# A product of the selective scan moved from VectorE to GpSimd, with B spread by loads from a DRAM copy

## The chip, the cores and the metric

The kernel runs on one core of a Trainium2 chip. The metric is the device time of one execution in microseconds: 5143.98 before the change, the median of three runs (5142.33 to 5146.24). The profile shown was taken of one execution, whose first to last instruction span 5146.1 us.

A core has five engines, each with a queue of its own that it works through in order: TensorE (PE in the profile; its weight loads are PEld), VectorE (DVE), ScalarE (ACT), GpSimd (POOL) and SyncE (SP), which here only issues transfers. SBUF is the working memory with 128 partitions, PSUM the memory that TensorE writes its sums into (eight banks of 128 x 512 f32), DRAM lies outside the core.

## The reference

The input is a batch of 8 images, 384 channels, 32 x 32 pixels, all in f32. Layer 0 normalises over channels, runs a selective scan (Mamba) over the 1024 pixels forward and backward, adds a gated depthwise 3 x 3 convolution and the input. Layer 1 is causal attention with rotary embedding and a feed-forward whose weights are Kronecker products. What the change touches is the scan:

```python
x_dbl = jnp.einsum('blc,ec->ble', u, x_proj_w)
dt, Bm, Cm = jnp.split(x_dbl, [dt_rank, dt_rank + D_STATE], axis=-1)
delta = jax.nn.softplus(jnp.einsum('blr,dr->bld', dt, dt_proj_w) + dt_proj_b)
A = -jnp.exp(A_log)
deltaA = jnp.exp(delta[..., None] * A)
deltaBu = (delta * u)[..., None] * Bm[:, :, None, :]

def step(h, inp):
    dA, dBu, c = inp
    h = dA * h + dBu
    return (h, jnp.einsum('bdn,bn->bd', h, c))
```

There are 16 state dimensions n. For each of them and each channel d, a recurrence runs over the tokens; B and C hold one number per token and n, the same for all channels.

## The kernel before

The kernel goes through the batch element by element. In layer 0 the channels lie on the partitions (384 = 3 groups of 128, called cc) and the tokens along the free dimension; in layer 1 tokens lie on the partitions. The scan of an element has four steps, each over a half of the tokens (512): forward first half, forward second half, backward second half, backward first half. Within a step `scan` loops over the 16 state dimensions, so that there are 8 x 4 x 16 = 512 state dimensions in all. For each one:

- ScalarE computes da = exp(delta A), three instructions (L331).
- VectorE computes hs = du * bb, one instruction over 3 x 512 elements (L333). du is delta times u; bb is row n of B, the same on every partition.
- VectorE runs the recurrence in place of hs, one `tensor_tensor_scan` for each channel group (L341). It reads da and hs, both in SBUF. In the first steps of each direction the last state is saved (L344).
- VectorE multiplies hs by cb, row n of C on every partition (L345).
- TensorE adds hs into the PSUM tile y with an identity as weights (L349); a product of f32 matrices shows as two records, so there are six for the three groups.

bb and cb come from TensorE: the tile bc holds B and C with tokens on the partitions, and four transposes of a column that is repeated 128 times make the row on all partitions, in PSUM (`spread`, L320). There is one PSUM bank for bb and one for cb, three for y and three for everything else (the tiles named w).

The work that doesn't belong to the running scan is written as generators, of which `pump` advances some pieces after each state dimension: the next step's `prepare` (the short convolution L256 and L264, B and C, and delta through a softplus, L292 to L302), the next element's `norm_in`, the gated convolution `local` (L213 to L231), and the previous element's attention and feed-forward (`tail`, three pieces at a time). The framework then orders each engine's instructions by its own estimate, so in the built program the recurrences of one state dimension are mixed with the product with C of the one before and with side work. GpSimd has, within the loop, only the copies of L499 for the feed-forward. SyncE issues the loads of x and the stores of the output.

Buffers that matter here: hs has three, da two (each for three groups), du one, dl (delta) two, tmp (work tiles of one group, in the softplus, the norm and `local`) four.

Of the kernel before, what the change touches and what calls it, by code (L numbers as in the profile page):

```python
"""Two layers of a vision backbone on one NeuronCore, batch element by batch element.

Layer 0 (bidirectional selective scan and gated depthwise convolution) works with channels on the
partitions; layer 1 (causal attention with rotary embedding, Kronecker-factored feed-forward) with
tokens on the partitions.  What an element needs stays in SBUF from its load to its store.

The scan runs in four steps for each element: forward over the first and the second half of the
tokens, then backward over the second and the first.  The work that does not belong to the scan
(the next step's projections, the next element's norm and input projection, the previous
element's layer 1) is issued in pieces between the state dimensions of the running step.  # L10
"""

# [13 lines left out]
P = 128  # L26
HB = 512  # tokens of a half
STEPS = [(0, 0), (0, 1), (1, 1), (1, 0)]  # (direction, half) in the order of the scan


@with_exitstack
def conv_attn_kernel(
# [29 lines left out]
    NF = cp1T.shape[0] // P  # L62
    NG = P // NJ  # row groups of the feed-forward's first factor
    NT = HB // P  # token tiles of a half
    HR = HB // W  # image rows of a half

# [4 lines left out]
    ps_b = ctx.enter_context(tc.tile_pool(name="ps_b", bufs=1, space=bass.MemoryType.PSUM))  # L71
    ps_w = ctx.enter_context(tc.tile_pool(name="ps_w", bufs=3, space=bass.MemoryType.PSUM))

# [8 lines left out]

    # ---------------------------------------------------------------- x comes first
    xv = x.rearrange("b (cc p) h w -> b p cc (h w)", p=P)
# [9 lines left out]

    # ---------------------------------------------------------------- constants and weights
    ident = const.tile([P, P], F32, name="ident")
# [33 lines left out]

    # A = -exp(A_log)
    nc.scalar.activation(nega, nega, AF.Exp)
    nc.vector.tensor_scalar_mul(nega, nega, -1.0)

    # D as diagonals
    ddiag = const.tile([P, NC, P], F32, name="ddiag")
    for cc in range(NC):
        nc.gpsimd.tensor_scalar(ddiag[:, cc], ident, v_d[:, cc : cc + 1], None, ALU.mult)

    # q, k weights with their rotated columns beside them  # L140
    qk = []
# [11 lines left out]
    sscale = 1.0 / K**0.5  # L153
    # sums the two stacked halves and gives the sum to both
    fold = const.tile([P, P], F32, name="fold")
# [3 lines left out]
    make_causal_mask(nc, cmask, -1e30)  # L159
    # the second factor of the feed-forward's output  # L160
    emat = const.tile([NJ, NJ, NI], F32, name="emat")
# [6 lines left out]

    # ---------------------------------------------------------------- layer 0: norm and input
    xn_t, u_t = {}, {}  # L170

    def norm_in(b, h):
# [9 lines left out]
        for cc in range(NC):  # L182
            nc.scalar.square(xn[:, cc, cols], xt[:, cc])
            nc.tensor.matmul(ms, ones, xn[:, cc, cols], start=cc == 0, stop=cc == NC - 1)
        rstd = l0.tile([P, HB], F32, tag="tmp", name=name("rstd"), bufs=4)
        nc.scalar.activation(rstd, ms, AF.Sqrt, bias=eps[:, 0:1], scale=1.0 / C)
# [17 lines left out]
    def local(b):  # L204
        """x + res_scale * sigmoid(dwconv(xn)) * xn, in place of x."""
        xn = xn_t[b]
        for cc in range(NC):
            img = xn[:, cc].rearrange("p (h w) -> p h w", w=W)
            for h in range(2):
                cols = slice(h * HB, (h + 1) * HB)  # L210
                sg = l0.tile([P, HB], F32, tag="tmp", name=name("sg"), bufs=4)
                sv = sg.rearrange("p (h w) -> p h w", w=W)
# [21 lines left out]
    def gate(b, h):  # L234
        """silu(z) of a half."""
        sz = l0.tile([P, NC, HB], F32, tag="sz", name=name("sz"))
        for m in range(NC):
            pz = bank()
            for cc in range(NC):
                nc.tensor.matmul(  # L240
                    pz, win[:, cc, C + m * P : C + (m + 1) * P],
                    xn_t[b][:, cc, h * HB : (h + 1) * HB],
                    start=cc == 0, stop=cc == NC - 1,
                )
            nc.scalar.activation(sz[:, m], pz, AF.Silu)
        return sz

    # ---------------------------------------------------------------- layer 0: the scan
    def prepare(b, step, res):
        """u after the convolution, B and C, delta of a step."""  # L250
        d, h = step
# [22 lines left out]
        yield  # L274
        # B and C with tokens on the partitions, from where transposes spread them
        pt = bank()
        for i in range(NT):
            nc.tensor.transpose(
                pt[:, i * NX : (i + 1) * NX], xd[:, i * P : (i + 1) * P], ident[:NX, :NX]
            )  # L280
        bc = l0.tile([P, NT, 2 * NS], F32, tag="bc", name=name("bc"), bufs=2)
        nc.scalar.copy(bc, pt[:, : NT * NX].rearrange("p (i e) -> p i e", i=NT)[:, :, R:])
        yield
        # softplus(v) = relu(v) + ln(1 + exp(-|v|))
        dl = l0.tile([P, NC, HB], F32, tag="dl", name=name("dl"), bufs=2)
        sps = []
        for cc in range(NC):
            pd = bank()
            nc.tensor.matmul(pd, dtw[:, cc * P : (cc + 1) * P], xd[:R], start=True, stop=True)
            sp = l0.tile([P, HB], F32, tag="tmp", name=name("sp"), bufs=4)  # L290
            bias = v_dtb[:, cc : cc + 1]
            nc.scalar.activation(sp, pd, AF.Abs, bias=bias)  # L292
            nc.scalar.activation(dl[:, cc], pd, AF.Relu, bias=bias)
            sps.append(sp)
            yield
# [5 lines left out]
        for cc, sp in enumerate(sps):  # L301
            nc.vector.tensor_add(dl[:, cc], dl[:, cc], sp)  # L302
        res.append((uc, bc, dl))

    carry = const.tile([P, NS, NC], F32, name="carry")

    def scan(step, prep, y, first, last, save, restore, pump):
        """One step: y += C . h + D u over the half's tokens."""
        d, h = step
        uc, bc, dl = prep  # L310
        du = l0.tile([P, NC, HB], F32, tag="du", name=name("du"))
        nc.vector.tensor_mul(du, dl, uc)
        for cc in range(NC):
            nc.tensor.matmul(y[:, cc], ddiag[:, cc], uc[:, cc], start=first, stop=False)  # L314

        def spread(what, at):
            """A column of bc as a row on every partition."""
            pb = ps_b.tile([P, HB], F32, tag=what, name=name(what))
            for i in range(NT):
                nc.tensor.transpose(  # L320
                    pb[:, i * P : (i + 1) * P],
                    bc[:, i, at : at + 1].to_broadcast([P, P]),
                    ident,
                )
            return pb.unsqueeze(1).to_broadcast([P, NC, HB])

        bb, cb = spread("bb", 0), spread("cb", NS)
        for n in range(NS):
            da = l0.tile([P, NC, HB], F32, tag="da", name=name("da"), bufs=2)
            for cc in range(NC):  # L330
                nc.scalar.activation(da[:, cc], dl[:, cc], AF.Exp, scale=nega[:, cc, n : n + 1])  # L331
            hs = l0.tile([P, NC, HB], F32, tag="hs", name=name("hs"), bufs=3)
            nc.vector.tensor_mul(hs, du, bb)  # L333
            if n + 1 < NS:
                bb = spread("bb", n + 1)
            for cc in range(NC):
                o, a = hs[:, cc], da[:, cc]
                if d:
                    o, a = o[:, ::-1], a[:, ::-1]
                init = carry[:, n, cc : cc + 1] if restore else 0.0  # L340
                nc.vector.tensor_tensor_scan(o, a, o, init, ALU.mult, ALU.add)  # L341
# [4 lines left out]
            if n + 1 < NS:  # L346
                cb = spread("cb", NS + n + 1)
            for cc in range(NC):
# [5 lines left out]
    def project(b, h, yz, t1):  # L354
        """The layer's output, tokens on the partitions: yz @ out_proj.T + x'."""
        for i in range(NT):
# [10 lines left out]

    # ---------------------------------------------------------------- layer 1
    def token_norm(t1, ti0):
        """1 / sd and -mean / sd of a half's tokens."""  # L370
        mv = l1.tile([P, NT, 2], F32, tag="mv", name=name("mv"))
# [20 lines left out]
    def attention(b, t1):  # L392
        k_all = l1.tile([P, L], F32, tag="k", name=name("k"))
        v_all = l1.tile([P, L // P, C], F32, tag="v", name=name("v"))
        for hh in range(2):
# [4 lines left out]
            for i in range(NT):  # L400
# [10 lines left out]
                yield  # L411
            # q as (q cos, q_rot sin), one above the other; k as their sum, twice
            def turned(w, nm):
# [74 lines left out]
    def feed_forward(b, t1):  # L488
        for hh in range(2):
            nrm = token_norm(t1, hh * NT)  # L490
            yield
            # the Kronecker factors' short dimension first, copied to each row group
            px = bank()
# [44 lines left out]

    # ---------------------------------------------------------------- the order of it all
    def run(gen):  # L540
# [7 lines left out]
    def pump_of(gens, each):  # L548
        """Advances the generators by so many pieces between two state dimensions."""

# [68 lines left out]
def _arrays(i):  # L619
    """The inputs, transposed and packed for the loads, and the table of rotary angles."""  # L620
    import numpy as np
# [67 lines left out]
```

## Time and profile before

| what | value |
|---|---|
| median of three runs | 5143.98 us (5142.33 to 5146.24) |
| the profiled execution's span | 5146.1 us |
| VectorE busy | 4576.4 us, 89% |
| TensorE busy | 4037.1 us, 78% |
| ScalarE busy | 2710.1 us, 53% |
| GpSimd busy | 37.1 us, 1% |
| product with C (L345), the last one's end | 4930.5 us |
| the four steps of a middle element | about 165, 176, 135 and 144 us |

How to read the profile. A group's line names the source line, the engine, the operation, the tile written and those read, the shapes and the number of instructions; then the group's busy time in us and the mean ns of one; then the engine's idle time just before these instructions and who ended most of it. The chain follows the work back from the end: at each step to what released an instruction, or to the one before it on its engine. A line of the windows view gives one stretch: its borders, its length, then busy us and number of instructions for PE, PEld, DVE, ACT and POOL, TensorE's granted clock, and the transfers' share. In the timeline the first number is the start in us, the second the duration. Records of neighbouring VectorE instructions overlap by some 0.08 us, so sums over records are a little higher than busy times.

### The profile page before, as it was taken

To read this page: it belongs to the slowest core of one execution; us is meant where nothing else is said; L and a number is where in the kernel's file an instruction comes from. 1 tells how busy PE (TensorE), PEld (TensorE's weight loads), DVE (VectorE), ACT (ScalarE), POOL (GpSimd) and SP (SyncE) were. 2 spreads that over 40 slices of the span, in tenths; PEclk is the share of its full clock that TensorE was granted. 3 is DMA by queue.
4 is the path that set the end of the run, shared out by engine and by line. 5 is a ranking of instruction groups with operands and counts; after the bars stand their busy time and mean duration, and the time that the engine had idled before them with its cause. 6 is when DMAs were issued, how large, how long until landed. Compare 5 with 4: busy or idle time off the path is not lost.

```text
span 5146.1 us, 35644 instructions
## 1 busy us (share of the span) xinstructions
PE 4037.1 (78%) x12656; PEld 1932.0 (38%) x12656; DVE 4576.4 (89%) x4788; ACT 2710.1 (53%) x3879; POOL 37.1 (1%) x75
## 2 busy tenths in 40 slices
PE   6667788778887788867888678877788777887677
PEld 2333343334433344333443334433343333433332
DVE  7998999989999899998998988998999989999841
ACT  4643557635575345744467445664456635575222
POOL 0000000000000000000000000000000000000000
PEclk8879899898988999999998899989999898988988
DMA  1000000000000000000000000000000000000000
GB/s 41 0 0 6 7 1 7 6 6 7 1 6 7 6 7 1 13 0 7 7 1 13 0 7 7 1 13 6 6 1 6 7 6 7 1 6 6 1 0 13
DMA packets 19255, 31.11 MB, mean 6 GB/s; under 512 B 5356, under 2 KB 6276, under 8 KB 19076
## 3 DMA queue, kind: packets, MB, share of 16 engines
q1 hardware_dynamic: 17152, 28.64, 1.6%
q8 instruction: 99, 1.62, 0.1%
q14 instruction: 80, 0.66, 0.0%
q10 hardware_dynamic: 1924, 0.19, 0.0%
HBM read 16.24 MB, written 12.58 MB: 6 GB/s over the span
## 4 chain that ended last, share of the span: by engine, by line
DVE 60%; PE 22%; issue 10%; ACT 8%; DMA 0%; ACTq 0%; POOL 0%; DVEq 0%; POOLq 0%
DVE hs L341 27%; DVE hs L333 11%; DVE hs L345 11%; PE y L349 4%; DVE uc L264 3%; PE w L360 3%; DVE sg L222 2%; PE w L240 2%; PE w L518 2%; PE w L479 2%; ACT da L331 2%; PE y L314 1%; PE w L512 1%; PE w L432 1%; ACT L331 1%
## 5 line engine op out<-in xcount | busy, mean ns | idle before, releaser
L349 PE MATMUL y<-hs,ident 128*128 128x512 f32 x3072 | 1637.3, 673 | 80.7 <-DVE hs L345 80.7
L331 ACT ACTIVATE da<-dl,nega 128x512 f32<-128x512 f32 x1536 | 1019.9, 714 | 1246.5 <-DVE hs L341 1052.8
L345 DVE TENSOR_TENSOR hs<-hs,cb 128x1536 f32<-128x1536 f32 x512 | 892.1, 1742 | 152.0 <-PE cb L320 146.9
L341 DVE TENSOR_TENSOR_SCAN hs<-da,carry,hs 128x512 f32<-128x512 f32 x768 | 937.6, 1265 | 8.6 <-ACT da L331 6.1
L341 DVE TENSOR_TENSOR_SCAN hs<-da,hs 128x512 f32<-128x512 f32 x768 | 900.8, 1209 | 3.6 <-ACT da L331 0.4
L333 DVE TENSOR_TENSOR hs<-du,bb 128x1536 f32<-128x1536 f32 x512 | 889.1, 1737 | 16.6 <-PE bb L320 16.3
L349 PEld LDWEIGHTS y<-hs,ident 128*128 128x128 f32 x3072 | 625.5, 219 | 710.0 <-issue 617.6
L320 PE MATMUL cb<-ident,bc 128*128 128x128 f32 x2048 | 370.5, 308 | 469.2 <-DVE hs L345 468.0
L320 PE MATMUL bb<-ident,bc 128*128 128x128 f32 x2048 | 336.9, 287 | 292.8 <-DVE hs L333 291.4
L320 PEld LDWEIGHTS cb<-ident,bc 128*128 128x128 f32 x2048 | 251.4, 151 | 668.4 <-DVE hs L345 593.0
L331 ACT ACT_TABLE_LOAD x275 | 352.8, 1283 | 246.3 <-DVE hs L341 213.1
L320 PEld LDWEIGHTS bb<-ident,bc 128*128 128x128 f32 x2048 | 237.1, 141 | 589.5 <-DVE hs L333 456.2
L222 DVE SCALAR_TENSOR_TENSOR sg<-xn,dww,sg 128x496 f32<-128x496 f32 (+3 forms) x384 | 273.3, 715 | 1.5
L479 PE MATMUL w<-v,pT 128*128 128x384 f32 x576 | 224.6, 540 | 27.5 <-ACT pT L475 27.5
L518 PE MATMUL w<-gl,cp1s 128*32 128x512 f32 x384 | 208.1, 658 | 37.9 <-ACT gl L517 36.8
L264 DVE SCALAR_TENSOR_TENSOR uc<-u,cw,uc 128x512 f32<-128x512 f32 (+3 forms) x288 | 210.6, 737 | 1.3
L512 PE MATMUL w<-xrT,fc1s 32*128 32x512 f32 x384 | 161.2, 686 | 39.7 <-ACT xrT L507 39.7
L479 PEld LDWEIGHTS w<-v,pT 128*128 128x128 f32 x576 | 114.8, 207 | 113.5 <-ACT pT L475 41.9
L360 PE MATMUL w<-wout,sz 128*128 128x384 f32 x384 | 140.1, 502 | 20.6 <-DVE sz L607 11.9
L517 ACT ACT_TABLE_LOAD x106 | 136.0, 1283 | 29.8 <-PE w L512 28.4
L517 ACT ACTIVATE gl<-w 128x512 f32<-128x512 f32 x192 | 107.5, 595 | 77.5 <-PE w L512 76.5
L267 ACT ACTIVATE uc<-uc 128x512 f32<-128x512 f32 x96 | 59.7, 629 | 151.7 <-DVE uc L264 151.4
(122 smaller groups left out, 3869.7 us busy)
## 6 DMA issues: line engine op xcount, KB each, us to landing
x<-in_x_dram SPq DMA_DIRECT2D x16, 768.0 KB, 4.5
out_dram<-os SPq DMA_DIRECT2D x48, 256.0 KB, 2.0
win<-in_in_wT_dram SPq DMA_DIRECT2D x1, 1152.0 KB, 9.1
wout<-in_out_wT_dram SPq DMA_DIRECT2D x1, 576.0 KB, 7.4
wvs<-in_wv_dram SPq DMA_DIRECT2D x1, 576.0 KB, 4.9
cs<-in_rope_dram SPq DMA_DIRECT2D x1, 512.0 KB, 4.9
fc1s<-in_fc_dram SPq DMA_DIRECT2D x1, 192.0 KB, 3.4
cp1s<-in_cp1T_dram SPq DMA_DIRECT2D x1, 192.0 KB, 2.8
```

Source lines behind the costliest of these rows:

```text
L222: nc.vector.scalar_tensor_tensor(o, img[:, r0 + dy : r1 + dy, c0 + dx : c1 + dx], dww[:, cc, k : k + 1], o, ALU.mult, ALU.add,)
L264: nc.vector.scalar_tensor_tensor(o, u[:, cc, a + s : e + s], cw[:, cc, k : k + 1], o, ALU.mult, ALU.add)
L320: nc.tensor.transpose(pb[:, i * P : (i + 1) * P], bc[:, i, at : at + 1].to_broadcast([P, P]), ident,)
L331: nc.scalar.activation(da[:, cc], dl[:, cc], AF.Exp, scale=nega[:, cc, n : n + 1])
L333: nc.vector.tensor_mul(hs, du, bb)
L341: nc.vector.tensor_tensor_scan(o, a, o, init, ALU.mult, ALU.add)
L345: nc.vector.tensor_mul(hs, hs, cb)
L349: nc.tensor.matmul(y[:, cc], ident, hs[:, cc], start=False, stop=last and n == NS - 1)
L360: nc.tensor.matmul(po[:, :C], yz[:, cc, cols], wout[:, cc], start=cc == 0, stop=False)
L479: nc.tensor.matmul(pa[:, :C], pT[:, j * P : (j + 1) * P], v_all[:, j], start=j == 0, stop=j == ti,)
L517: nc.scalar.activation(gl, ph, AF.Gelu)
L518: nc.tensor.matmul(po[:NJ], cp1s[:, f], gl, start=f == 0, stop=f == NF - 1)
```

## The change

The product of du and B goes to GpSimd, which works in SBUF alone; so B has to be spread over the partitions in SBUF. `prepare` stores the 16 rows of B of a step (xd, with tokens along the free dimension) to a DRAM tile bd, and `scan` loads two rows at a time onto all 128 partitions (bbt, two buffers, 512 KB for each load). The transposes for bb go. du is computed at the end of `prepare` of the step ahead and has two buffers. The bank that bb had goes to the side work (three to four). For room in SBUF, tmp goes from four buffers to three, bc holds C alone, and da becomes a tile for each group with four buffers. In the changed file comments are gone, and lines are moved by a few.

```diff
+NB2 = 2
-    ps_w = ctx.enter_context(tc.tile_pool(name="ps_w", bufs=3, space=bass.MemoryType.PSUM))
+    dram = ctx.enter_context(tc.tile_pool(name="dram", bufs=1, space=bass.MemoryType.DRAM))
+    ps_w = ctx.enter_context(tc.tile_pool(name="ps_w", bufs=4, space=bass.MemoryType.PSUM))
...
-        rstd = l0.tile([P, HB], F32, tag="tmp", name=name("rstd"), bufs=4)
+        rstd = l0.tile([P, HB], F32, tag="tmp", name=name("rstd"), bufs=3)
...
+        bd = dram.tile([NS, HB], F32, tag="bd", name=name("bd"), bufs=2)
+        nc.sync.dma_start(bd, xd[R : R + NS])
...
-        bc = l0.tile([P, NT, 2 * NS], F32, tag="bc", name=name("bc"), bufs=2)
-        nc.scalar.copy(bc, pt[:, : NT * NX].rearrange("p (i e) -> p i e", i=NT)[:, :, R:])
+        bc = l0.tile([P, NT, NS], F32, tag="bc", name=name("bc"), bufs=2)
+        nc.scalar.copy(bc, pt[:, : NT * NX].rearrange("p (i e) -> p i e", i=NT)[:, :, R + NS :])
...
-        res.append((uc, bc, dl))
+        du = l0.tile([P, NC, HB], F32, tag="du", name=name("du"), bufs=2)
+        nc.vector.tensor_mul(du, dl, uc)
+        res.append((uc, bc, bd, dl, du))
...
-        uc, bc, dl = prep
-        du = l0.tile([P, NC, HB], F32, tag="du", name=name("du"))
-        nc.vector.tensor_mul(du, dl, uc)
+        uc, bc, bd, dl, du = prep
...
-        bb, cb = spread("bb", 0), spread("cb", NS)
+        cb = spread(0)
         for n in range(NS):
-            da = l0.tile([P, NC, HB], F32, tag="da", name=name("da"), bufs=2)
-            for cc in range(NC):
-                nc.scalar.activation(da[:, cc], dl[:, cc], AF.Exp, scale=nega[:, cc, n : n + 1])
+            if n % NB2 == 0:
+                bbt = l0.tile([P, NB2, HB], F32, tag="bb", name=name("bb"), bufs=2)
+                nc.sync.dma_start(
+                    bbt, bd[n : n + NB2].rearrange("(o k) t -> o k t", o=1).to_broadcast([P, NB2, HB])
+                )
+            das = []
+            for cc in range(NC):
+                da = l0.tile([P, HB], F32, tag="da", name=name("da"), bufs=4)
+                nc.scalar.activation(da, dl[:, cc], AF.Exp, scale=nega[:, cc, n : n + 1])
+                das.append(da)
             hs = l0.tile([P, NC, HB], F32, tag="hs", name=name("hs"), bufs=3)
-            nc.vector.tensor_mul(hs, du, bb)
-            if n + 1 < NS:
-                bb = spread("bb", n + 1)
+            nc.gpsimd.tensor_mul(hs, du, bbt[:, n % NB2].unsqueeze(1).to_broadcast([P, NC, HB]))
             for cc in range(NC):
-                o, a = hs[:, cc], da[:, cc]
+                o, a = hs[:, cc], das[cc]
```

## The prediction

> **What bounds the kernel now.** I read the shares by engine first, then the chain of waits, then the groups, then stretches of one batch element.
>
> ```profile
> span 5146.1 us, 35644 instructions
> ...
> PE 4037.1 (78%) x12656; PEld 1932.0 (38%) x12656; DVE 4576.4 (89%) x4788; ACT 2710.1 (53%) x3879; POOL 37.1 (1%) x75
> ...
> DVE 60%; PE 22%; issue 10%; ACT 8%; DMA 0%; ACTq 0%; POOL 0%; DVEq 0%; POOLq 0%
> ...
> L345 DVE TENSOR_TENSOR hs<-hs,cb 128x1536 f32<-128x1536 f32 x512 | 892.1, 1742 | 152.0 <-PE cb L320 146.9
> L341 DVE TENSOR_TENSOR_SCAN hs<-da,carry,hs 128x512 f32<-128x512 f32 x768 | 937.6, 1265 | 8.6 <-ACT da L331 6.1
> L341 DVE TENSOR_TENSOR_SCAN hs<-da,hs 128x512 f32<-128x512 f32 x768 | 900.8, 1209 | 3.6 <-ACT da L331 0.4
> L333 DVE TENSOR_TENSOR hs<-du,bb 128x1536 f32<-128x1536 f32 x512 | 889.1, 1737 | 16.6 <-PE bb L320 16.3
> ```
>
> VectorE is busy 89% and carries 60% of the chain; GpSimd is empty. Three quarters of VectorE's time are the scan's own: the product with B (L333), three recurrences (L341), the product with C (L345). The windows below are the four scan steps of the third element, in order, with the bare tail last.
>
> ```profile
> core 0: us, PE busy (x) PEld busy (x) DVE busy (x) ACT busy (x) POOL busy (x), PEclk, DMA share, GB/s
> 1350.00:1516.00 166.00, 142.50 (x456) 66.94 (x455) 152.68 (x186) 119.81 (x169) 4.43 (x8) 0.92 0.01 5
> 1516.00:1692.00 176.00, 132.06 (x392) 57.35 (x391) 167.16 (x162) 95.44 (x125) 0.00 (x0) 0.88 0.01 5
> 1692.00:1828.00 136.00, 105.19 (x333) 52.16 (x334) 118.45 (x95) 62.99 (x89) 0.00 (x0) 0.92 0.02 6
> 1828.00:1972.00 144.00, 120.29 (x408) 64.10 (x408) 133.18 (x156) 65.33 (x108) 0.00 (x0) 0.94 0.02 6
> ...
> 4930.00:5146.00 216.00, 166.40 (x467) 74.16 (x466) 39.58 (x106) 61.58 (x118) 3.08 (x8) 0.85 0.02 8
> ```
>
> In each step VectorE is the fullest engine. Its idle time is 13.3 + 8.8 + 17.5 + 10.8 = 50.4 us per element, 403 us for eight.
>
> **What GpSimd does beside VectorE.** This is the row that decides for me. The only GpSimd work in the loop is a small copy (L499). Two places from the timeline, GpSimd first, then VectorE at the second of them:
>
> ```profile
> 862.16 0.30 POOL L499 COPY xr<-xr 128x128 f32<-128x128 f32 x1 [0.63 <-DVE xr L498]
> ...
> 739.05 1.16 POOL L499 COPY xr<-xr 128x128 f32<-128x128 f32 x1 [2.04 <-DVE xr L498]
> ```
> ```profile
> 738.90 1.22 DVE L341 TENSOR_TENSOR_SCAN hs<-da,hs 128x512 f32<-128x512 f32 x1
> ```
>
> At 862.16 VectorE runs L333, whose second operand lies in PSUM, and the copy takes 0.30. At 739.05 it runs a recurrence, with both operands in SBUF: the copy ends at 740.20, 0.09 after the recurrence (740.12). Of the 64 copies, 26 meet no VectorE instruction with two SBUF operands and take 0.294 to 0.298; the other 38 (L341, L222, L496) all end 0.09 to 0.16 after it. So GpSimd does not read while such an instruction runs, and it does get in between two back-to-back recurrences. The recurrence behind the copy took 1.246 against 1.195 for the one after it: a hint that VectorE waits in its turn, no proof, as the copy is so short.
>
> **The change part by part.**
>
> *The product with B leaves VectorE.* 512 x 1.737 = 889 us, and the 17 us it waited for bb: -906. TensorE loses 512 x 4 transposes (337 us) and their weight loads; they lie beside VectorE's work: 0. With no cover left, a step could not fall below TensorE's own work (142.5 less 10.5 in the first).
>
> *It goes to GpSimd as a product of two SBUF tensors, 128x1536.* No such row exists. A memset of one element takes 0.10, of 128 elements 0.205 (0.83 ns per element); the undisturbed copy 0.295 (1.52 ns); the multiplication by a column, L138, 0.606 (3.95 ns). Lower end, at the copy's pace: 1536 x 1.52 + 0.1 = 2.4 us. Upper end, at L138's: 6.2. I take the copy plus a second operand read at the memset's pace, 2.35 ns: 3.6 us held (0.1 of start is over by then), nearest to the copy because a tensor product has no column operand. GpSimd has 512 x 3.6 = 1843 us of work, far from full.
>
> *What it makes VectorE wait.* Recurrences (1838 us), convolutions (L222, L264) and some 260 us more read two SBUF tensors; L345 reads PSUM. A product that holds the operand path beside L345 covers some 1.66 us of itself; before a recurrence it covers nothing. When does it start? It needs an hs buffer. There are three, and the order of the changed program is: two recurrences of n+1, L345 of n, the third recurrence. So product n+3 waits until TensorE has read hs of n: 0.65 for cb's transposes and 2.74 for six y matmul records, 3.28 after L345's end in the undisturbed case, some 3.4 with the signal. Follow one state dimension without side work, from L345's end, recurrences at 1.17 pace, L345 1.66. No wait at first: recurrences end at 3.5, the request falls at 3.4 inside the third, GpSimd starts at 3.5 beside L345 and ends at 7.1, L345 at 5.17: the next recurrence waits 1.94. Now the recurrences stand at 1.94, 3.10, 4.27: the request at 3.4 falls in the second, GpSimd starts at 4.27, the third waits 3.6 in full, and L345 later finds GpSimd idle. Then it repeats: mean (1.94 + 3.6) / 2 = 2.77 us. As a check over all steps I took, in the trace of before, each of the 512 ends of y's matmuls, let GpSimd start at the end of the two-SBUF instruction running there, and counted how much of 3.5 us the following VectorE work outside that class does not cover: mean 2.70. I take 2.70: 512 x 2.70 = +1382. By the lower price (2.4) the same count gives 1.68, +860; by the upper 5.33, +2729.
>
> *Cover by idle time.* While VectorE stands, TensorE and ScalarE catch up (L345 waits 147 us for cb). I take half of the 403 us: -200; ends 0 and -403.
>
> *B through DRAM.* 32 stores of 32 KB and 256 spread loads of 512 KB on SP's queue. The 768 KB loads of x land in 4.5 us; a load is issued when GpSimd releases a pair, one pair (some 20 us) ahead: 0, once +7 at the start, where store (2.0 for 256 KB) and load stand in a row. On SP's queue each load waits for GpSimd, and stores of the output and x loads stand behind it, at most a product late; the output store holds a gl buffer for that long, which delays a gelu, not VectorE: 0. If loads took two state dimensions' time, every second product would wait.
>
> *Delta u one step ahead.* 32 x 1.74 = 56 us, still on VectorE: 0; between -56, if all stood at a step's head, and +56, if it now delays recurrences.
>
> *Buffers.* da apart with four (VectorE waits 6.5 us for it): 0. tmp from four to three, shared by the softplus and the gated convolution: 0 to +37 (L229's present wait for ScalarE). One more PSUM bank for the side work: 0 to -8 (L455's wait). Half the copy to bc: 0. The 64 xr copies now queue behind products, up to 3.6 us each, which delays transposes of the feed-forward that TensorE's 22% idle time covers: 0.
>
> Sum against the profiled execution (span 5146.1, nothing visible around it; 2.1 above the median 5143.98, 0.04%): 5146 - 906 + 1382 - 200 + 7 = 5429, rounded 5430.
>
> *The skill beside these rows.* The Trainium skill, SBUF — State Buffer, section "Who interferes with whom", says the port pair of VectorE and GpSimd is an exclusive lock for a whole instruction, in either direction, also for a VectorE instruction with two SBUF inputs. The trace shows the one direction 38 times; the other only by the 0.05 above. By the rule the sum is the one here; if only GpSimd waited, it would be near 4400. The GPSIMD Engine Reference, section 3.1, measures 4497 ns for a tensor product of 2048 elements, by which 1536 take an estimated 3.4 us; the alternation then gives 2.57 per product and a sum of 5363 (an estimate). It advises VectorE for such work.
>
> **The rivals.** All turn on one number: the change pays while a product costs VectorE less than (906 + 200) / 512 = 2.16 us.
>
> 1. *The hold falls beside L345* (faster). If the request comes in the last recurrence before L345 or during it each time, the wait is 3.6 - 1.66 = 1.94: 5146 - 906 + 993 - 200 = 5033, with all idle time covered 4830, none 5233. For it: 1.94 is a lasting state where the request comes 0.9 us later, and in loaded steps y ends 5.5 us after L345 on average. Against: then two or three side instructions with two SBUF operands stand before L345 as well.
> 2. *VectorE does not wait, or the product is as short as 2.4* (faster). Steps shrink by 21 (TensorE's bound), 28, 28, 28 us: 8 x 105 = 840, 4306; with 860 of waits less 200, 4900. For it: only one direction is plainly seen. Against: the recurrence stretched behind the copy.
> 3. *The product is slower* (far slower). At 4.5 us some 3.65 of wait: 5146 - 906 + 1869 - 300 = 5809; at 6.2, 5146 - 906 + 2729 - 403 = 6566. For it: L138's pace. Against: L138 has a column operand.
>
> **How the numbers follow.** The forecast, both wait and 3.6: 52%, its own range 5230 (all idle covered) to 5630 (none). Rival 1: 22%, 4830 to 5230. Rival 2: 12%, 4310 to 4900. Rival 3: 14%, above 5630. Slower: 52 + 14 and 2 of rival 1 = 68%; within 0.2% (what these runs can tell from nothing) 3%; faster 29%. The range leaves out most of rival 2 and the upper part of rival 3: 4780 to 5800.
>
> **What would show it.** Right: GpSimd's product near 3.6, longer in records where it waits at its start; recurrences whose records or gaps grow to several us with GpSimd as neighbour, L345 unchanged at 1.74; VectorE's own wait for hs small; loads landing in 3 to 5 us. Wrong: recurrences still 1.2 to 1.27 with GpSimd busy beside them; a product of 2.5 or of 5 us; VectorE waiting for DMA or for TensorE in place of GpSimd.

## The result and the profile after

The changed kernel takes 5676.61 us (median of four runs, 5665.8 to 5681.93) against 5143.15 (four runs, 5141.65 to 5146.24) of the one before: a ratio of 1.1035, 95% interval 1.1019 to 1.105. It is 533 us slower. The prediction was 5430, range 4780 to 5800.

The page of the profile after, in the order in which the page before was read: shares by engine, the chain, the groups of the scan.

```profile
span 5678.2 us, 32493 instructions
...
PE 3970.0 (70%) x10608; PEld 1812.4 (32%) x10608; DVE 4976.3 (88%) x4276; ACT 2831.4 (50%) x3920; POOL 1966.8 (35%) x587
...
DVE 64%; issue 19%; PE 7%; ACT 6%; POOL 3%; DMA 0%; ACTq 0%; DVEq 0%; POOLq 0%
...
L345 POOL TENSOR_TENSOR hs<-du,bb 128x1536 f32<-128x1536 f32 x512 | 1928.1, 3771 | 3286.7 <-PE y L359 2866.3
...
L351 DVE TENSOR_TENSOR_SCAN hs<-da,carry,hs 128x512 f32<-128x512 f32 x768 | 1371.2, 1818 | 86.3 <-POOL hs L345 54.6
L351 DVE TENSOR_TENSOR_SCAN hs<-da,hs 128x512 f32<-128x512 f32 x768 | 1170.3, 1562 | 83.8 <-POOL hs L345 83.8
...
L355 DVE TENSOR_TENSOR hs<-hs,cb 128x1536 f32<-128x1536 f32 x512 | 888.8, 1736 | 210.4 <-PE cb L325 206.5
...
L354 DVE COPY carry<-hs 128x3 f32<-128x3 f32 x256 | 259.1, 1012 | 1.7
...
bb<-bd SPq DMA_DIRECT2D x256, 512.0 KB, 3.6
```

VectorE gave up 889 us of work and yet is busy 400 us longer. The instructions that it kept are the same and their records have grown: the recurrence from 1265 and 1209 ns to 1818 and 1562, the saving of the carry from 160 to 1012. The product with C, which reads PSUM, is unchanged (1736). GpSimd is idle 65% of the span, so it is no bound by its own work; the loads land in 3.6 us and are nobody's wait.

The timeline shows how a record grows. GpSimd's second product first, then its neighbours:

```profile
1862.67 4.15 POOL L345 TENSOR_TENSOR hs<-du,bb 128x1536 f32<-128x1536 f32 x1
```
```profile
1859.10 3.43 POOL L345 TENSOR_TENSOR hs<-du,bb 128x1536 f32<-128x1536 f32 x1 [7.67 <-PE y L359]
1859.23 4.38 DVE L351 TENSOR_TENSOR_SCAN hs<-da,hs 128x512 f32<-128x512 f32 x1
```
```profile
1863.64 3.21 DVE L354 COPY carry<-hs 128x3 f32<-128x3 f32 x1
```

A product starts at 1859.10 and ends at 1862.53. The recurrence issued 0.13 us behind it ends at 1863.61, 1.08 after the product: it ran when the product was over. The next product, issued at 1862.67, takes 4.15 instead of 3.4, for it first stood behind that recurrence; and the copy of three numbers per partition stood behind it in its turn until 1866.85. Of 1536 recurrences 245 are longer than 2 us; of the 256 carry copies 70 are longer than 1 us. An undisturbed product takes 3.41. Of the 374 VectorE instructions with two SBUF operands whose records start inside a product's (more than 0.05 us after its start, more than 0.15 before its end), 360 end after the product; the other 14 ran first, and the products that they held took 4.5 to 4.9 us.

The windows below are one batch element by its true scan steps, in the kernel before and then after.

```profile
1228.86:1393.82 164.96, 143.49 (x499) 77.70 (x500) 149.24 (x188) 90.32 (x149) 1.58 (x2) 0.97 0.02 5
1393.82:1570.36 176.54, 154.75 (x476) 65.64 (x474) 168.05 (x191) 126.11 (x165) 2.86 (x6) 0.90 0.03 9
1570.36:1706.13 135.77, 91.51 (x270) 42.77 (x270) 128.06 (x122) 61.06 (x83) 0.00 (x0) 0.87 0.00 0
1706.13:1849.84 143.71, 109.04 (x338) 53.97 (x338) 126.11 (x102) 65.04 (x92) 0.00 (x0) 0.91 0.02 6
```
```profile
1375.57:1555.33 179.76, 144.41 (x427) 73.64 (x427) 150.65 (x169) 93.41 (x146) 59.95 (x19) 0.89 0.09 31
1555.33:1749.85 194.52, 150.93 (x421) 61.76 (x421) 187.05 (x186) 129.25 (x171) 62.56 (x22) 0.86 0.08 28
1749.85:1893.02 143.17, 85.02 (x200) 37.82 (x200) 142.79 (x100) 65.59 (x85) 58.99 (x17) 0.81 0.08 30
1893.02:2065.08 172.06, 109.99 (x278) 51.60 (x278) 141.38 (x84) 70.27 (x93) 65.02 (x17) 0.79 0.08 29
```

The third number of each row, after the length and PE and PEld, is VectorE's busy time. Every step is longer, by 15, 18, 7 and 28 us. VectorE's idle time is 15.7, 8.5, 7.7, 17.6 before (49.5 in all) and 29.1, 7.5, 0.4, 30.7 after (67.6): it grew, where the prediction let it cover part of the waits.

### The profile page after: what moved, and what is told of

It reads as the page before. It is cut to its first block, busy times and chain, and to the rows that moved or that the text cites. A ratio compares the mean times of both kernels' runs of the same rounds, so it can differ in the third digit from the quotient of the medians.

```text
span 5678.2 us, 32493 instructions
## 1 busy us (share of the span) xinstructions
PE 3970.0 (70%) x10608; PEld 1812.4 (32%) x10608; DVE 4976.3 (88%) x4276; ACT 2831.4 (50%) x3920; POOL 1966.8 (35%) x587
## 4 chain that ended last, share of the span: by engine, by line
DVE 64%; issue 19%; PE 7%; ACT 6%; POOL 3%; DMA 0%; ACTq 0%; DVEq 0%; POOLq 0%
DVE hs L351 32%; DVE hs L355 10%; DVE sg L224 5%; DVE uc L266 4%; DVE carry L354 4%; POOL hs L345 3%; PE y L359 2%; ACT da L342 1%; DVE sg L231 1%; DVE uc L258 1%; PE w L442 1%; DVE du L309 1%; DVE xn L192 1%; PE w L528 1%; DVE dl L307 1%
## 5 line engine op out<-in xcount | busy, mean ns | idle before, releaser
L345 POOL TENSOR_TENSOR hs<-du,bb 128x1536 f32<-128x1536 f32 x512 | 1928.1, 3771 | 3286.7 <-PE y L359 2866.3
L359 PE MATMUL y<-hs,ident 128*128 128x512 f32 x3072 | 1810.6, 729 | 113.2 <-DVE hs L355 113.2
L351 DVE TENSOR_TENSOR_SCAN hs<-da,carry,hs 128x512 f32<-128x512 f32 x768 | 1371.2, 1818 | 86.3 <-POOL hs L345 54.6
L351 DVE TENSOR_TENSOR_SCAN hs<-da,hs 128x512 f32<-128x512 f32 x768 | 1170.3, 1562 | 83.8 <-POOL hs L345 83.8
L355 DVE TENSOR_TENSOR hs<-hs,cb 128x1536 f32<-128x1536 f32 x512 | 888.8, 1736 | 210.4 <-PE cb L325 206.5
L224 DVE SCALAR_TENSOR_TENSOR sg<-xn,dww,sg 128x496 f32<-128x496 f32 (+3 forms) x384 | 366.2, 964 | 0.7
L266 DVE SCALAR_TENSOR_TENSOR uc<-u,cw,uc 128x512 f32<-128x512 f32 (+3 forms) x288 | 293.0, 1032 | 2.1
L354 DVE COPY carry<-hs 128x3 f32<-128x3 f32 x256 | 259.1, 1012 | 1.7
L273 PE MATMUL w<-uc,xp 128*56 128x512 f32 x192 | 109.9, 689 | 144.8 <-ACT uc L269 144.7
L199 PE MATMUL w<-xn,win 128*128 128x512 f32 x288 | 149.7, 667 | 42.7 <-DVE xn L192 42.7
L370 PEld LDWEIGHTS w<-wout,sz 128*128 128x128 f32 x384 | 82.5, 231 | 172.2 <-DVE sz L617 124.2
```

The costliest lines, as they stand in the source:

```text
L224: nc.vector.scalar_tensor_tensor(o, img[:, r0 + dy : r1 + dy, c0 + dx : c1 + dx], dww[:, cc, k : k + 1], o, ALU.mult, ALU.add,)
L266: nc.vector.scalar_tensor_tensor(o, u[:, cc, a + s : e + s], cw[:, cc, k : k + 1], o, ALU.mult, ALU.add)
L345: nc.gpsimd.tensor_mul(hs, du, bbt[:, n % NB2].unsqueeze(1).to_broadcast([P, NC, HB]))
L354: nc.vector.tensor_copy(carry[:, n], hs[:, :, at])
L355: nc.vector.tensor_mul(hs, hs, cb)
L359: nc.tensor.matmul(y[:, cc], ident, hs[:, cc], start=False, stop=last and n == NS - 1)
```

## The experiments

The theory under test, called the held path in the expectations: a GpSimd product and a VectorE instruction that both read SBUF exclude each other for their whole length, in both directions. Rivals: the loads and buffers cost the time; VectorE merely waits for products that come late.

### The product back on VectorE, all else as changed

```diff
-            nc.gpsimd.tensor_mul(hs, du, bbt[:, n % NB2].unsqueeze(1).to_broadcast([P, NC, HB]))
+            nc.vector.tensor_mul(hs, du, bbt[:, n % NB2].unsqueeze(1).to_broadcast([P, NC, HB]))
```

> Everything of the change stays (DRAM copy of B, spread loads, buffers, delta u ahead), only the product goes back to VectorE, now with both operands in SBUF. Theory 'held path' (a VectorE instruction and a GpSimd instruction that both read SBUF exclude each other for their whole length): recurrences back at 1.20 to 1.27 us, product 1.74, time 5030 to 5160, as 512 x 1.74 = 889 us come back and 1228 us of lengthened VectorE records go. Rival 'loads and buffers' (134 MB written into SBUF, three tmp buffers, four da tiles are the cost): VectorE's records stay long and the time stays above 5400.

Measured: 4985.45 us, ratio to the kernel before 0.9702 (0.9678 to 0.9725), faster than the 5030 to 5160 expected. The groups of VectorE in its trace:

```profile
L351 DVE TENSOR_TENSOR_SCAN hs<-da,carry,hs 128x512 f32<-128x512 f32 x768 | 945.8, 1268 | 34.8 <-ACT da L342 33.0
L351 DVE TENSOR_TENSOR_SCAN hs<-da,hs 128x512 f32<-128x512 f32 x768 | 899.6, 1208 | 1.8
L355 DVE TENSOR_TENSOR hs<-hs,cb 128x1536 f32<-128x1536 f32 x512 | 890.4, 1739 | 126.0 <-PE cb L325 125.1
L345 DVE TENSOR_TENSOR hs<-du,bb 128x1536 f32<-128x1536 f32 x512 | 890.0, 1740 | 6.6 <-PE y L359 6.6
```

The recurrences are back at 1268 and 1208 with the same 134 MB of loads beside them, so loads and buffers do not lengthen them. The rest of the change even gains: this kernel beats both, by 3% and by 12%. The move of the product to GpSimd alone costs 5677 - 4985 = 691 us, and the rest of the change gains 158.

### GpSimd writes as long, and reads nothing

Left out: delta u times B; the scan runs on zeros.

```diff
-            nc.gpsimd.tensor_mul(hs, du, bbt[:, n % NB2].unsqueeze(1).to_broadcast([P, NC, HB]))
+            nc.gpsimd.memset(hs, 0.0)
+            nc.gpsimd.memset(hs, 0.0)
+            nc.gpsimd.memset(hs[:, 0], 0.0)
```

> In place of the product GpSimd fills hs with zeros by three memsets (two of 1536 elements, one of 512; about 3.3 us by the memset rows), so it writes SBUF as long but reads nothing. Left out: delta u times B, so the scan runs on zeros. Held path: only a GpSimd instruction that reads is in the way, recurrences 1.20 to 1.27, VectorE's records lose 1228 us; by the prediction's sum without waits 4300 to 4650. If writes exclude VectorE too, records stay near 1.7 on average and the time above 5300. Rival 'late hs' (VectorE is late because the products come late through three hs buffers): as GpSimd takes as long, the time stays above 5300 too, but with waits between records and not longer records.

Measured: 4477.85 us, ratio 0.8709 (0.8688 to 0.873). Groups of VectorE, then of GpSimd:

```profile
L353 DVE TENSOR_TENSOR_SCAN hs<-da,carry,hs 128x512 f32<-128x512 f32 x768 | 948.6, 1267 | 80.2 <-POOL hs L347 34.3 <-POOL hs L346 27.1 <-ACT da L342 18.7
L353 DVE TENSOR_TENSOR_SCAN hs<-da,hs 128x512 f32<-128x512 f32 x768 | 897.8, 1207 | 33.8 <-POOL hs L346 27.5 <-PE w L416 4.5 <-ACT da L342 1.4
...
L356 DVE COPY carry<-hs 128x3 f32<-128x3 f32 x256 | 113.1, 442 | 3.1
```
```profile
L346 POOL MEMSET hs<- 128x1536 f32 x512 | 711.4, 1390 | 29.1
L345 POOL MEMSET hs<- 128x1536 f32 x512 | 708.2, 1383 | 2283.1 <-PE y L361 2155.9 <-DVE uc L258 72.4 <-DVE hs L353 39.3
L347 POOL MEMSET hs<- 128x512 f32 x512 | 271.7, 531 | 28.7
```

GpSimd is occupied for 3.3 us per state dimension as with the product, through the same three hs buffers, and 1199 us are gone; VectorE's records fell from 5270 to 4123 us, its idle time from 702 to 674. So neither late hs nor GpSimd's being busy is the cost: its reading is. The recurrences run at their old lengths beside writes. The carry copy doesn't (442 against 160 ns), nor does L258, a multiplication of one tensor by columns (673 against 532): these read a single tensor and still wait for a GpSimd that only writes.

The Trainium skill, SBUF — State Buffer, section "Who interferes with whom", makes this distinction: a VectorE instruction with two SBUF inputs collides with a GpSimd instruction that reads SBUF and not with one that only writes, while copies and tensor-scalar operations, where they run in a two-port mode, collide with GpSimd without that distinction. The lengths agree, with 1267 and 1207 ns beside writes for the first kind and 442 and 673 for the second; that the second kind ran in such a mode is shown by no run here.

### The product done twice

```diff
             nc.gpsimd.tensor_mul(hs, du, bbt[:, n % NB2].unsqueeze(1).to_broadcast([P, NC, HB]))
+            nc.gpsimd.tensor_mul(hs, du, bbt[:, n % NB2].unsqueeze(1).to_broadcast([P, NC, HB]))
```

> The same product is done twice, one after the other, into the same hs. Held path: a hold of 2 x 3.42 us for each state dimension of which only some 1.7 can lie beside the product with C; 512 x (about 5 more than now minus what new idle time covers) gives 6900 to 7500. Rival 'late hs' or 'loads and buffers': GpSimd is idle 65% of the time, so a second product of 3.4 us mostly fits into its idle time and costs at most 0.6 us each, below 6000.

Measured: 7050.91 us, ratio 1.3713 (1.368 to 1.3745). 1374 us more than the changed kernel, for 512 further products of 3.41 us (1746 us): 79% of a hold ends up in the time, though GpSimd had 3700 us to spare. Late results and loads as the cost are excluded by this one too.

### One operand of the recurrence moved out of SBUF

```diff
-    ps_w = ... bufs=4
+    ps_w = ... bufs=3
-                da = l0.tile([P, HB], F32, tag="da", name=name("da"), bufs=4)
+                if cc == DAP:
+                    da = ps_b.tile([P, HB], F32, tag="dap", name=name("dap"))
+                else:
+                    da = l0.tile([P, HB], F32, tag="da", name=name("da"), bufs=4)
```

> The da of the third channel group is written to a PSUM bank (taken from the side work's four), so a third of the recurrences read one operand from SBUF and one from PSUM, as the product with C does; results are the same. Held path: those recurrences do not wait, 1.2 to 1.35 us each, and a product can lie beside the product with C and the recurrence behind it, 2.9 us instead of 1.7; the wait per product falls from 2.40 to about 1.6, time 5150 to 5450. Rival 'VectorE waits for any GpSimd read whatever it reads': no recurrence is exempt and the time stays at 5650 to 5800.

Measured (DAP = 2): 5558.01 us, ratio 1.0816 (1.0791 to 1.084). VectorE's groups, those with da in SBUF and those with da in PSUM (dap):

```profile
L355 DVE TENSOR_TENSOR_SCAN hs<-da,carry,hs 128x512 f32<-128x512 f32 x512 | 890.3, 1751 | 72.8 <-POOL hs L349 58.5 <-ACT da L346 14.0
...
L355 DVE TENSOR_TENSOR_SCAN hs<-da,hs 128x512 f32<-128x512 f32 x512 | 797.7, 1574 | 155.8 <-POOL hs L349 155.7
L355 DVE TENSOR_TENSOR_SCAN hs<-dap,carry,hs 128x512 f32<-128x512 f32 x256 | 321.8, 1257 | 0.0
L355 DVE TENSOR_TENSOR_SCAN hs<-dap,hs 128x512 f32<-128x512 f32 x256 | 306.9, 1199 | 3.3 <-ACT dap L346 3.3
```

The same instruction on the same tile, with GpSimd as neighbour: all 512 with an operand in PSUM take 1.186 to 1.278 us, the 110 among them that ran wholly inside a product's record too; those with both in SBUF 1.66 on average and up to 4.5. That is the plainest proof of the mechanism. The expected gain was missed, 119 us in place of 226 to 526: records shrink by 252 us in all (5270 to 5018), but VectorE's idle time grows by 115 (702 to 817), and other instructions take over part of the wait (the softplus addition from 876 ns to 1370).

With the second and third groups in PSUM and two banks left for the side work:

> GpSimd computes the product as in the changed kernel; the da of the second and third channel groups lie in PSUM (one bank each, the side work is left two of its four). Held path: two thirds of the recurrences exempt at 1.2 to 1.3 us; the wait per product falls further, but one group and the side work still read two SBUF tensors, and the first step showed that waits move to them: 5250 to 5500 unless the two banks choke the side work. Rival 'only a change of place': every exempt instruction hands its wait to the next one in full, and the time stays at 5500 to 5600.

Measured: 5667.16 us, ratio 1.1019 (1.0997 to 1.1041); neither theory had it. The records go on falling (4816), the exempt recurrences stay at 1.23, but idle time rises to 1129: 322 us of waiting for GpSimd's hs, 123 for ScalarE's da in its single bank. How much of this the two missing banks make is not separated.

### A third of the product

```diff
-            nc.gpsimd.tensor_mul(hs, du, bbt[:, n % NB2].unsqueeze(1).to_broadcast([P, NC, HB]))
+            bb = bbt[:, n % NB2].unsqueeze(1)
+            nc.gpsimd.tensor_mul(hs[:, 2:], du[:, 2:], bb)
+            nc.vector.tensor_mul(hs[:, :2], du[:, :2], bb.to_broadcast([P, 2, HB]))
```

> GpSimd computes the product for the third channel group alone (128x512, a hold of some 1.15 us), VectorE for the other two (128x1024, some 1.2 us), B from SBUF for both. VectorE gives up 0.53 us per state dimension. Held path: if the wait keeps the whole product's share (2.4 of 3.42), it is 0.8 us and the time is 5080 to 5150, slower than 4985; if the short hold mostly lies beside the product with C, 0.3 us, and the time is 4850 to 4930. Theory 'GpSimd is simply twice as slow and VectorE only waits for late results': VectorE's records stay at their lengths and the time falls by up to 270 us, to about 4720.

Measured: 5158.8 us, ratio to the kernel before 1.003 (1.0019 to 1.0042), and 173 us slower than with the whole product on VectorE; it is just above the 5080 to 5150 expected for a wait that keeps its share. VectorE's other records grow by some 265 us for the 240 it gives up, and it is idle 118 us longer. Even a short hold costs more than the work it takes away.

### The start pinned beside the product with C

The prediction's first rival, made to happen: a copy of one element ties the product of n+1 to the end of the third recurrence of n, and ScalarE saves the carry.

```diff
+            if prev is not None:
+                nc.gpsimd.tensor_copy(t[:, 0, 0:1], prev[:, 2, 0:1])
+            nc.gpsimd.tensor_mul(t, du, bbts[0][:, n % NB2].unsqueeze(1).to_broadcast([P, NC, HB]))
...
                 nc.vector.tensor_tensor_scan(o, a, o, init, ALU.mult, ALU.add)
+                if cc == 2 and n + 1 < NS:
+                    nxt_hs = product(n + 1, hs)
...
-                nc.vector.tensor_copy(carry[:, n], hs[:, :, at])
+                nc.scalar.copy(carry[:, n], hs[:, :, at])
```

> GpSimd's product for state dimension n+1 is tied to the end of the third recurrence of n by a copy of one element per partition, so that it starts beside the product with C, and the saving of the carry goes to ScalarE; otherwise the changed kernel. This is the prediction's first rival made to happen. Held path: without side work a state dimension takes 3.5 (recurrences) + 1.66 (product with C) + about 2.0 (3.4 and the copy, less 1.66) = 7.2 us against 7.9 in the prediction's alternation; the time falls below 5676 by some 250 to 450 us, to 5220 to 5430, and recurrences longer than 2 us become rare, their wait now standing as VectorE's wait for hs. If the start does not matter, 5600 to 5750.

Measured: 5315.03 us, ratio 1.0334 (1.0318 to 1.035), within the expectation.

```profile
L361 DVE TENSOR_TENSOR_SCAN hs<-da,carry,hs 128x512 f32<-128x512 f32 x768 | 970.2, 1300 | 261.3 <-POOL hs L345 190.8 <-ACT da L353 57.2 <-ACT sp L297 8.8
L361 DVE TENSOR_TENSOR_SCAN hs<-da,hs 128x512 f32<-128x512 f32 x768 | 942.3, 1273 | 345.7 <-POOL hs L345 345.6
```

The recurrences are nearly at their own length, and the wait stands openly before them: 536 us for the product. Of the 512 products, 349 now lie 1 us or more beside a product with C, against 90 in the changed kernel. The two edits together bring 362 us. How much of it is the start of the product, and how much the saving of the carry, whose copies took 259 us of VectorE in the changed kernel, was not separated. It is not enough to win.

Starting one recurrence earlier, with the third one's da in PSUM (in a bank of the side work's four), so that 2.9 us of VectorE's work should lie beside the hold:

> As the kernel before this one, but the product starts at the end of the second recurrence, and the da of the third lies in PSUM: the third recurrence and the product with C (1.2 + 1.66) lie beside the hold of 3.4. Held path: a state dimension without side work takes 2.4 + 3.4 + 0.3 = 6.1 us, against 6.87 in the kernel before and with the product on VectorE; over all steps, where side work with two SBUF operands still waits, 4800 to 5100. If pinning costs more in late products than it saves, above 5300.

Measured: 5330.98 us, ratio 1.0365 (1.035 to 1.038); the expectation of a win fell, and the time is that of its other branch, above 5300. The recurrences are nearly free (1.285 us on average with da in SBUF, 1.229 with da in PSUM), but the side work, whose place among the recurrences this edit does not fix, now does the waiting: all scalar-tensor-tensor instructions (L225, L267 and the like) take 982 us in place of 628 with the product on VectorE, the softplus additions 1844 ns each in place of 677, and VectorE waits 327 us for the product.

### Where the 158 us of the rest come from

Each edit is made to the kernel with the product on VectorE (4985). Three banks for the side work again:

> The product on VectorE from B in SBUF (4985), but with the side work's PSUM banks back at three; the fourth is left empty. If the fourth bank is what makes that kernel faster than the one before, the time goes back to 5100 to 5143; if it is TensorE's relief from the transposes and their waits, it stays at 4975 to 5010.

Measured: 4995.94, ratio 0.9712 (0.9696 to 0.9728). du at the head of the step again:

> The product on VectorE from B in SBUF (4985), but du is computed at the head of the scan step again, with one buffer. If du one step ahead is the gain, the time rises by up to 32 x 1.74 = 56 us to about 5040; the prediction's term of zero says 4975 to 5000.

Measured: 4990.58, ratio 0.9703 (0.9689 to 0.9718). Three banks, and the transposes that spread B done again into the free bank, unread:

> The product on VectorE from B in SBUF with three banks for the side work (4996), and TensorE again does the 4 transposes per state dimension that spread B, into the free bank, where nobody reads them. If that kernel is 150 us faster than the one before because TensorE is relieved, the time goes back to 5100 to 5145; if it is faster because VectorE's product no longer waits for TensorE and the order of the work differs, it stays at 4980 to 5030.

Measured: 4987.09, ratio 0.9694 (0.9677 to 0.971). Three banks, du late, and da as one tile of three groups, without those transposes:

> The product on VectorE from B in SBUF, and every companion edit taken back at once but the three tmp buffers: du at the head of the step, three banks for the side work, da as one tile of three groups with two buffers. If da's own tiles are the gain of 150 us, the time goes back to 5100 to 5145. If the gain is that VectorE's product and TensorE's queue no longer wait for each other over bb's bank, it stays at 4980 to 5020.

Measured: 5012.55, ratio 0.9744 (0.9727 to 0.976).

What TensorE waited for, in the kernel before:

```profile
PE bb L320 <- DVE hs L333: 291.4, 190, 8.1
```

The bank, du and TensorE's relief are worth nothing that shows; with all companion edits taken back but the three tmp buffers and the copy of C alone to bc, 27 of the 158 us go. About 133 us remain for B's lying in SBUF when VectorE needs it: in the kernel before, TensorE stood 291 us before the spreading of bb until VectorE had read the previous row, with other work queued behind; with the unread transposes this wait is gone. That this wait is the cause is by elimination, not shown by itself; that the framework orders the work otherwise in these kernels is not excluded.

## Why the prediction was right, and where its sum was off

The direction, the range and the mechanism held; the size was about half (287 us forecast, 533 measured). The measured 5677 lies above the forecast's own 5230 to 5630, where the prediction had put only a slower product (rival 3), and that is not what happened. Two misses of opposite sign stand behind it, the wait put 134 us too high and the cover by idle time 332 us off the other way, so that the total is as near as it is owes something to luck.

- *The row that decided.* Reading 38 small GpSimd copies that ended 0.09 to 0.16 us after a VectorE instruction with two SBUF operands, and taking a recurrence lengthened by 0.05 as a hint of the other direction, was right. The write-only run, the doubled product and the recurrences with an operand in PSUM show that VectorE waits; the products behind a recurrence in the changed kernel's trace (4.15 us in place of 3.41) show that GpSimd does.
- *The product, 3.6 us held.* Measured 3.41; the rows' construction was 6% high. The estimate of 3.4 that the prediction draws from the Trainium skill's GPSIMD Engine Reference, section 3.1, was closer; the page's 4497 ns is measured on an addition, not on a product.
- *2.70 us of wait for each product, +1382.* VectorE's records grew by 5270 - (4911 - 889) = 1248 us, 2.44 each; 71% of a hold against the 75% assumed (2.70 of 3.6). The size was nearly right, the picture behind it was not: the alternation puts every second product beside a product with C, but in the trace 90 of the 512 lie 1 us or more beside one and 346 do not touch one. That the mean came out near is in part luck. The class was drawn wrongly, too: the carry copy (+218 us) and L256's multiplication (+37) were counted as not affected, since they read one tensor.
- *Cover by idle time, -200.* This step failed. VectorE's idle time rose from 570 to 702 us: it waits 138 us for hs and 206 (before: 147) for cb. Against the kernel with the product on VectorE (452 idle) it is +250. The likely reason is that the engines wait for each other in a ring: while VectorE stands behind a product, the products with C come later, and so do y, the hs buffers and the next products (GpSimd waits 2866 us for y's matmuls to release hs). This is read from the waits; no run tested it by itself, with more hs buffers for instance. The term was put at -200 and measured +132, so it was 332 us off, more than the whole miss of 246 (533 - 287).
- *B through DRAM and the buffers, +7.* Measured with the product on VectorE it is -158: a gain that the product's move hid. The term of -906 had taken the coupling to TensorE at its 17 us of direct waiting; what it costs TensorE's queue was not priced, and by the elimination above, not by a test, some 133 us belong there.
- *Rival 1* (hold beside L345) was priced at 5033; made to happen for 349 of the products, and with the carry copies gone from VectorE, it gives 5315, as late products (536 us of waiting) and waiting side work eat the rest. *Rival 2* (VectorE doesn't wait) was put at 4306, and elsewhere in the prediction at "near 4400" without a sum; the write-only run, 4478, is the nearest thing to it. *Rival 3* (slower product) is excluded by 3.41.
- The stretches called scan steps in the prediction began some 120 us late and cut across steps; their sum covers a whole element, so the 403 us of idle time stands (49.5 per element by the true borders), the split by step does not.

## What to carry to other kernels

Before work goes from VectorE to GpSimd, sort VectorE's instructions by where their operands lie: in these runs what reads two SBUF tensors stood still for the whole of a GpSimd instruction that reads SBUF, one with an operand in PSUM didn't, and the small copies and L258's multiplication, which read one SBUF tensor, waited too. By this the offload pays only if a GpSimd instruction's length, less what is sure to lie beside it, is below the time it takes off VectorE. Test the parts of a change apart: here the companion edits were worth 3%, and the headline edit cost 14% of the kernel they make. And do not let idle time pay for a new wait when the idle engine's partners depend on it through a few buffers.

## What the runs showed of the hardware that was not expected

- A VectorE copy of three numbers per partition, 0.16 us, can take 3.2 us behind a GpSimd instruction, and it waits for GpSimd's writes as well as for its reads (mean 442 ns beside memsets, 1012 beside products).
- TensorE's mean granted clock differed between the kernels: 0.927 at 82% busy (write only, where its sums run over zeros), 0.913 at 78% (before), 0.832 at 70% (after), 0.769 at 58% (twice). Its busy share alone does not set it: with the product on VectorE and three banks it was 0.872, at 78% as well. The matmul records of y took 729 ns on average in the changed kernel in place of 673, though they are the same matmuls. What this adds to the time was not separated.
